# Another order of the stages for the second layer, and its weights loaded four pieces ahead, in a two-layer local-attention kernel

## The chip, the cores and the metric

The kernel runs on one core of one Trainium2 chip. The metric is the device time of one launch in microseconds (us), the median of several runs. Engines are called PE (TensorE; PEld is its loading of weights), DVE (VectorE), ACT (ScalarE), POOL (GpSimd) and SP (SyncE, which here only issues transfers). [...]

## What is computed

The input x is 8 sequences of 1024 tokens with 256 features, all in float32. Cut to what matters:

```python
x = layernorm(x + causal_attention(x, wq, bq, wk, bk, wv, bv, wo, bo))   # one head of 64
y = x
for l in range(2):                                 # two layers, 8 heads of 64, hidden width 682
    h = shift_token(y)                             # second half of the features from the token before
    q, k, v = split(h @ wqkv[l])
    q, k = rotary_xpos(l2norm(q) * q_scale[l], l2norm(k) * k_scale[l])
    o = local_attention(q, k, v)                   # a window of 128 tokens sees itself and the one before
    y = y + o @ wo[l]
    h = layernorm(shift_token(y)) * ln_g[l] + ln_b[l]
    a, g = split(h @ w1[l] + b1[l])
    y = y + (a * gelu(g)) @ w2[l] + b2[l]
x = layernorm(x + y)
```

## The kernel before

**Arithmetic.** To keep float32 accuracy, a matrix product is made of three passes: each operand is split into a high part (`hi`, a rounded copy by ACT) and the rest (`lo`, a subtraction by DVE or POOL), and hi*hi, hi*lo and lo*hi are added up in PSUM (`products`, L93). Weights are split once, by `split_weight` (L184 to L189), after a load into a staging tile.

**Three parts.** `fronts` runs the first attention for all sequences (to about 277 us). Then `layers` runs the two layers as one long loop, and the end of the loop is the end of the kernel. Layer 1 reads what layer 0 has written to DRAM (`x1_d`), and adds the input of layer 0 (`x0_d`) and the last layernorm.

**The loop.** Tiles of 128 tokens are numbered w = 0 to 127: 64 of layer 0, then 64 of layer 1. Round j (j = 0 to 66) works around w = 2j. It goes through a hand-written list, `ORDER`, whose entries are (stage, offset to w, and sometimes a half). The stages of a tile are:

- `prep` (once for two tiles): loads x (L670), transposes it (l_xp) and splits it (l_xT);
- `qk` (halves 0 and 1) and `v`: the projections l_pqk and l_pv; for `qk` the Square l_sq (L754) and its sum l_ss (L757), and the rotation l_t (L764, L771) with the table l_tab (L746); for `v` a copy l_v (L792);
- `unit`: the norms of q and k, a power on POOL (L144), and k's scaling (L782);
- `turn`: transposes q and k (l_t) into the ring of keys and queries;
- `sc`: the scores l_sc, their masked minimum on DVE (L843) and the exponential l_e on ACT (L703); after the second half the reciprocals of the denominators go to DRAM (L860) and come back spread over the partitions as `R` (L866);
- `et`: transposes l_e (eight transposes a half) and copies them, l_eT (L885);
- `val`: values times l_eT into one bank, l_po;
- `out`: l_on = l_po * R (L909), split into l_oT (L914, L915);
- `proj`: l_py, and its sum with x (L927).

After the `proj` of an odd tile, the feed-forward of the two tiles is put into a queue; each ("side", 1) in the list advances it by one of eleven steps: the shifted rows m_sh by transfers (L947 to L954) and the normalisation m_hn (L152, L153, L144, L964); the transposes m_hp; six steps m_pag with gelu on ACT (L703) and its product (L1013 to L1017); two steps m_pf; and the end, x (L1043), in layer 1 with the final norm o_st, o_mv (L1052). Both lists, old and new, have eleven sides.

**What sets the order on the engines.** The program text gives priorities; the Tile scheduler orders each engine's instructions at compile time, from the readiness that it simulates. On PE there is one more rule (`queued`, L114): the matmuls that use half of the array (`sc` and `val`) form groups that stay in program order with all the others before and behind them. Within a stretch between two such groups the scheduler is free. Buffers are counted by tag in `sizes`; "ps" (four banks) serves every PE result but the scores, which have four half-filled banks of their own ("sc").

**Weights of layer 1.** They share tiles with those of layer 0, one buffer each, so a split can start only when the last matmul of layer 0 that reads the old ones is done. Each piece is loaded into a staging tile of tag "sq", which is also that of the Squares, right where it is split: `load_qkv` when the first `prep` of layer 1 is traced (round 31), `load_wo` after the last `proj` of layer 0 (round 33), `load_w1` and `load_w2` inside the last feed-forward of layer 0. `load_b1` works out layer 1's b1 in rounds 1 and 2, and stages its pieces in "sq" too.

```python
        for j in range(PAIRS + 3):
            w = 2 * j
            if j >= 1:
                next(later, None)
            for item in ORDER:
                if item[0] == "side":
                    side(item[1])
                else:
                    run(item[0], w + item[1], *item[2:])
```

Of the kernel before, what the change touches and what calls it, by code (L numbers as in the profile page):

```python
# [9 lines left out]
FP = mybir.dt.float32  # L10
FR = mybir.dt.float32r
AF = mybir.ActivationFunctionType
ALU = mybir.AluOpType
# [13 lines left out]
def kernel(  # L27
# [544 lines left out]
    def load_w1(l, stage, W, ps=None):  # L572


        if ps is not None:
            b1_tiles(l, W)
        lgb, full = W["lgb"], NF * P
        W["w1"] = pair([P, 2, CW], "w1", wpool)
        gap = slice(2 * full + LEFT, 2 * full + OFF)
        for t in W["w1"]:  # L580
            nc.gpsimd.memset(t[:, :, gap].bitcast(FP), 0.0)
        for c in range(2):
            if ps is not None:
                pb = ps(f"pb1_{l}_{c}")
            for k, m0, m1, st in w1_parts(l, stage, c):
                if ps is not None:
                    b1_part(W, pb, c, k, m0, m1, st)
                nc.vector.tensor_scalar(st, st, lgb[:, 0, c : c + 1], None, ALU.mult)
                n = min(m1, NF) - m0
                s3 = st[:, 0 : n * P].rearrange("p (m q) -> p m q", q=P)  # L590
                d3 = [
                    t[:, c, 0 : 2 * full].rearrange("p (m k q) -> p m k q", k=2, q=P)[
                        :, m0 : m0 + n, k, :
                    ]
                    for t in W["w1"]
                ]
                split_weight(d3[0], d3[1], s3)
                if m1 > NF:
                    o = 2 * full + k * OFF
                    split_weight(  # L600
                        W["w1"][0][:, c, o : o + LEFT], W["w1"][1][:, c, o : o + LEFT],
                        st[:, n * P : n * P + LEFT],
                    )
                yield
            if ps is not None:
                b1_add(W, pb)

    def load_w2(l, stage, W):
# [22 lines left out]
        W["b2"] = b2t  # L631
        yield

    QB = 4
    PSB = {"ps": 4, "sc": 4}
    ORDER = [
        ("qk", 0, 0), ("unit", -2), ("unit", -1), ("side", 1), ("turn", -2, 0), ("side", 1),
# [4 lines left out]
        ("val", -2, 0), ("val", -2, 1), ("et", -1, 1), ("side", 1), ("qk", 1, 1),  # L642
        ("val", -1, 0), ("val", -1, 1), ("side", 1), ("side", 1), ("side", 1),
    ]

    def layers(pool, psum):
        sizes = {
            "sq": 4, "t": 6, "v": 4, "eT": 2, "oT": 2, "on": 1, "R": 2, "xT": 4, "hT": 2, "hn": 1,
            "sh": 3, "a": 10, "gl": 3, "x": 6, "tab": 2,
        }  # L650

        def tl(tag, shape, name, dt=FP):
            return pool.tile(shape, dt, tag=tag, name=name, bufs=sizes[tag])
# [3 lines left out]

        def sm(shape, tag, name, bufs=4, dt=FP):
            return pool.tile(shape, dt, tag=tag, name=name, bufs=bufs)

        def ps(name):
            return psum.tile([P, 512], FP, tag="ps", name=name, bufs=PSB["ps"])
# [274 lines left out]
        def feed_forward(l, b, p, x1, W):  # L937
# [82 lines left out]
            if change:  # L1020
                for _ in later:
                    pass
                for _ in load_w1(l + 1, stage, Ws[l + 1]):
                    pass
            py = ps(f"{nm0}_pf")
            for i in range(2):
                cols = slice(i * P, (i + 1) * P)
# [9 lines left out]
                passes(py[:, i * E : (i + 1) * E], steps)  # L1037
                yield
            if change:
                for _ in load_w2(l + 1, stage, Ws[l + 1]):  # L1040
                    pass
            xf = x1.rearrange("p t e -> p (t e)")
            nc.vector.tensor_tensor(xf, py, xf, ALU.add)  # L1043
            if not last_layer:
# [26 lines left out]
        def run(name, w, *args):  # L1071

            if not 0 <= w < DEPTH * B * NT:
                return
            l, b, t = w // (B * NT), w // NT % B, w % NT
            if (l, b) not in A:
                if "wqk" not in Ws[l]:
                    for _ in load_qkv(l, stage, Ws[l]):
                        pass
                W = Ws[l]  # L1080

                def finished(p, xt):
                    queue.append(feed_forward(l, b, p, xt, W))

                A[l, b] = attention(l, b, W, finished)
            A[l, b][name](t // 2 if name == "prep" else t, *args)
            if name == "proj" and b == B - 1 and t == NT - 1 and l + 1 < DEPTH:
                for _ in load_wo(l + 1, stage, Ws[l + 1]):
                    pass

        PAIRS = DEPTH * B * NT // 2
        group["on"] = True
# [15 lines left out]
        while queue:  # L1108
            side(1)

# [66 lines left out]
```

## Time and profile before

| What | Value |
| --- | --- |
| Median of 3 runs (lowest, highest) | 2683.63 us (2682.82, 2688.84) |
| The profiled execution's own time | 2688.53 us |
| Its span, first to last instruction | 2686.7 us |
| Mean granted clock of PE in it | 0.986 |
| PE, PEld busy | 2615.7 us, 2330.3 us |
| DVE, ACT, POOL busy | 2059.4, 1721.2, 1743.0 us |
| Matmuls | 22336 |

Times inside the kernel are those of one profiled execution, counted from its first instruction. Its own time is 1.8 us more than its span and 4.9 us more than the median. "L703" is line 703 of the kernel; a helper's line (L130 for every product, L133 for transposes, L90 and L91 for splits, L144 for powers) stands for many places, so tiles tell more than lines. In a list of waits, "PE l_et L133 <- ACT l_v L792" means that PE stood idle ahead of an l_et transpose until ACT's l_v copy was done; the numbers are the total, the count and the longest, in us. Matmuls are pipelined, so the times of neighbours overlap, and a matmul that starts late can still count as busy.

### The profile page before, as it was taken

Reading aid. Unit: us, or ns where it says so; the run is one execution under the profiler, and the core shown is the slowest. Engines: PE = TensorE matmul, PEld = TensorE weight load, DVE = VectorE, ACT = ScalarE, POOL = GpSimd, SP = SyncE. Lnnn points to the kernel's source line nnn. Section 1 sums busy time; section 2 is a strip of 40 time slices with the busy share of each in tenths; the row PEclk is TensorE's granted clock in tenths of the full one; section 3 lists DMA queues with packets and bytes.
Section 4 is the critical chain, followed back from the end, with each engine's and each line's share of the span. In section 5 each row is a group of like instructions: output and inputs, shape, how many; then the busy total and the mean of one; then the engine's idle time right before and its main releaser. Section 6 shows DMA issues by size and latency. Waiting matters only on the chain.

```text
span 2686.7 us, 61674 instructions
## 1 busy us (share of the span) xinstructions
PE 2615.7 (97%) x22336; PEld 2330.3 (87%) x22336; DVE 2059.4 (77%) x6304; ACT 1721.2 (64%) x4486; POOL 1743.0 (65%) x1996
## 2 busy tenths in 40 slices
PE   7998899999999999999999999999999999999997
PEld 5776799999999999999988888988888988889887
DVE  5787677777777777777778878887787877787775
ACT  5676466666666666666676666666666666666653
POOL 4565566666666666666666776676766767667673
PEclk8999899999999999999999999999999999999998
DMA  6332211111111111111121211111111111111110
GB/s 180 99 95 72 75 35 45 45 43 41 39 35 45 45 43 42 41 33 43 45 63 51 67 52 51 41 43 50 52 50 45 39 50 52 51 44 43 47 45 25
DMA packets 147265, 141.12 MB, mean 53 GB/s; under 512 B 28808, under 2 KB 123408, under 8 KB 146960
## 3 DMA queue, kind: packets, MB, share of 16 engines
q1 hardware_dynamic: 145600, 136.72, 17.4%
q8 instruction: 176, 2.88, 0.5%
q14 instruction: 129, 1.06, 0.1%
q10 hardware_dynamic: 1360, 0.46, 0.1%
HBM read 96.74 MB, written 27.81 MB: 46 GB/s over the span
## 4 chain that ended last, share of the span: by engine, by line
PE 65%; DVE 15%; POOL 8%; ACT 6%; issue 3%; DMA 2%; SPq 0%; POOLq 0%; DVEq 0%; ACTq 0%
PE m_pag L130 16%; PE l_pqk L130 10%; PE l_po L130 8%; PE l_et L133 6%; PE m_pf L130 6%; PE l_sc L130 4%; PE l_py L130 4%; PE l_pv L130 3%; ACT l_e L703 3%; PE l_t L133 3%; DVE l_t L764 2%; POOL l_t L771 2%; DVE l_ss L757 2%; DVE ring L91 2%; POOL l_oT L915 1%
## 5 line engine op out<-in xcount | busy, mean ns | idle before, releaser
L703 ACT ACTIVATE l_e<-l_sc,l_nm 128x256 f32<-128x256 f32 (+1 forms) x992 | 456.9, 481 | 216.8 <-DVE o_mv L153 107.7
L130 PE MATMUL m_pag<-m_hT,w_h 128*128 128x256 f32 (+1 forms) x2816 | 529.4, 288 | 0.7 <-ACT m_hT L90 0.7
L771 POOL TENSOR_TENSOR l_t<-l_t,l_t 128x256 f32<-128x256 f32 x512 | 369.8, 743 | 241.5 <-DVE l_t L764 241.5
L843 DVE CUSTOM_DVE_ANT_0 l_sc<-l_sc,mask,l_nrm_y 128x256 f32<-128x256 f32 (+1 forms) x1024 | 429.1, 466 | 45.8 <-ACT l_e L703 36.9
L130 PEld LDWEIGHTS m_pag<-m_hT,w_h 128*128 128x128 f32 (+1 forms) x2816 | 433.6, 188 | 17.7 <-issue 10.6
L703 ACT ACTIVATE m_gl<-m_pag,b 128x256 f32<-128x256 f32 (+1 forms) x384 | 181.9, 474 | 348.6 <-PE m_pag L130 348.5
L130 PE MATMUL m_pag<-m_hT,w_l 128*128 128x256 f32 (+1 forms) x1408 | 395.9, 281 | 0.0
L130 PE MATMUL l_pqk<-wqk_h,l_xT 128*128 128x512 f32 x1024 | 381.7, 414 | 1.4 <-ACT l_xT L90 0.8
L144 POOL TENSOR_TENSOR l_nrm_y<-l_nrm_a,half 128x16 f32<-128x16 f32 x128 | 373.6, 2918 | 10.5
L885 ACT COPY l_eT<-l_et 128x512 f32<-128x512 f32 (+1 forms) x512 | 274.5, 565 | 144.2 <-PE l_po L130 91.4
L764 DVE TENSOR_TENSOR l_t<-l_pqk,l_tab 128x512 f32<-128x512 f32 x512 | 327.3, 681 | 0.0
L1013 DVE SCALAR_TENSOR_TENSOR m_gl<-m_pag,b,m_gl 128x256 f32<-128x256 f32 (+1 forms) x384 | 183.6, 478 | 130.2 <-ACT m_gl L703 129.9
L133 PE MATMUL l_et<-ident,l_e 128*128 128x128 f32 x1920 | 266.3, 281 | 12.6 <-DVE l_cx L733 5.4
L1017 POOL TENSOR_TENSOR m_a<-m_gl,m_a 128x256 fp32r<-128x256 f32 x320 | 233.2, 735 | 54.3 <-DVE m_a L1016 53.0
L130 PEld LDWEIGHTS m_pag<-m_hT,w_l 128*128 128x128 f32 (+1 forms) x1408 | 264.0, 188 | 0.0
L133 PEld LDWEIGHTS l_et<-ident,l_e 128*128 128x128 f32 x1920 | 211.4, 141 | 58.6 <-DVE l_cx L733 12.5
L130 PE MATMUL m_pf<-w_h,m_a 128*128 128x256 f32 x1280 | 250.3, 282 | 0.0
L757 DVE TENSOR_REDUCE l_ss<-l_sq 128x8 f32<-128x512 f32 x256 | 175.1, 684 | 86.5 <-ACT l_sq L754 82.8
L130 PE MATMUL l_po<-l_eT,l_v 128*64 128x128 f32 x3840 | 239.5, 277 | 0.0
L130 PEld LDWEIGHTS l_po<-l_eT,l_v 128*64 128x64 f32 x3840 | 208.4, 137 | 34.1 <-issue 14.1
L142 POOL TENSOR_SCALAR l_nrm_a<-l_ss 128x16 f32<-128x16 f32 x128 | 32.3, 252 | 305.2 <-DVE l_ss L757 303.7
L130 PEld LDWEIGHTS l_pqk<-wqk_h,l_xT 128*128 128x128 f32 x1024 | 194.9, 190 | 38.1 <-DVE l_on L909 1.5
(168 smaller groups left out, 6704.8 us busy)
## 6 DMA issues: line engine op xcount, KB each, us to landing
l_R<-rd_d SPq DMA_DIRECT2D x256, 128.0 KB
x<-x_d SPq DMA_DIRECT2D x96, 256.0 KB
l_tab<-tab_d SPq DMA_DIRECT2D x128, 128.0 KB
xin<-in_L_attn_x_dram SPq DMA_DIRECT2D x16, 512.0 KB
x_d<-xin SPq DMA_DIRECT2D x16, 512.0 KB
rd_d<-l_rT SPq DMA_DIRECT2D x512, 1.0 KB
x_d<-x SPq DMA_DIRECT2D x32, 256.0 KB
out_dram<-x SPq DMA_DIRECT2D x32, 256.0 KB
```

The source lines that it names most:

```text
L91: nc.vector.tensor_tensor(lo, src, hi.bitcast(FP), ALU.subtract)
L130: queued(nc.tensor.matmul(*args, **kw), part)
L133: queued(nc.tensor.transpose(*args), False)
L144: nc.gpsimd.tensor_tensor(r, a, half.to_broadcast([P, n]), ALU.pow)
L703: ins = nc.scalar.activation(*args, **kw)
L757: nc.vector.tensor_reduce(st["ss", t][:, k * HEADS : (k + 1) * HEADS], sq.rearrange("p (g d) -> p g d", d=DH), AX.X, ALU.add)
L764: nc.vector.tensor_tensor(tt[j].rearrange("p (k h d) -> p k h d", k=2, d=DH), p3, tb.unsqueeze(2).to_broadcast([P, 2, HEADS // 2, DH]), AL ...
L771: nc.gpsimd.tensor_add(a[:, :, s, :], a[:, :, s, :], bsw[:, :, 1 - s, :])
L843: nc.vector.tensor_tensor_reduce(dst, dst, mk, st["nrm", w][:, 8 * u + h : 8 * u + h + 1], BIG, ALU.add, ALU.min, nm[:, one],)
L885: nc.scalar.copy(eT[:, j, 0:m], pt[:, 0:m])
L1013: nc.vector.scalar_tensor_tensor(gl[0:z, :], a_ps, W["b1"][0:z, 0, m : m + 1], gl[0:z, :], ALU.add, ALU.mult)
L1017: nc.gpsimd.tensor_tensor(a[1], gl[0:z, :], a[0].bitcast(FP), ALU.subtract)
```

## The change

Four things change, all in `layers`, beside new functions for the pieces.

1. A second list, `ORDER_1`, is used from round 33 on (`SWITCH`). In it a round's second tile gets its scores at the end of the round, and its `et`, `val`, `out` and `proj` in the next. At the switch two rounds of the new list are run without sides for what the old list has not yet done, which is `out` and `proj` of tile 62, and then two sides (`CATCH`). A set `done` keeps a stage from being run twice.
2. The weights of layer 1 are cut into 22 pieces (six of wqkv, two of wo, eight of w1, six of w2) by `parts_of`. Each is loaded into a tile of the new tag "ws", four buffers. The first four loads are issued after the `prep` of tiles 62 and 63 (round 30); later ones each when a piece before it is split. The splits stand where the whole loads stood.
3. To make room, "sq" has 2 buffers instead of 4, "R" 1 instead of 2, "sh" 2 instead of 3. This holds for both layers.
4. `load_b1` still stages in "sq".

```diff
+    def parts_of(l, W):
+        def from_rows(src):
+            def load(st):
+                nc.sync.dma_start(out=st, in_=src)
+            return load
+        def qkv(c, k):
+            def split(st):
+                if "wqk" not in W:
+                    t = pair([P, 2, 2, 2, INNER // 2], "wqk", wpool)
+                    W["parts"] = t
+                    W["wqk"] = [u.rearrange("p c g k f -> p c (g k f)") for u in t]
+                    W["wv"] = pair([P, 2, INNER], "wvv", wpool)
+                if k < 2:
+                    s3 = st.rearrange("p (g f) -> p g f", g=2)
+                    split_weight(*[u[:, c, :, k, :] for u in W["parts"]], s3)
+                else:
+                    split_weight(*[u[:, c, :] for u in W["wv"]], st)
+            src = wqkv[l, c * P : (c + 1) * P, k * INNER : (k + 1) * INNER]
+            return ("qkv", INNER, from_rows(src), split)
...
+        parts = [qkv(c, k) for c in range(2) for k in range(3)]
+        parts += [out_rows(c) for c in range(0, INNER // P, 2)]
+        cut = ((0, NF - 1), (NF - 1, NF + 1))
+        parts += [w1_piece(c, k, *m) for c in range(2) for k in range(2) for m in cut]
+        return parts + [w2_rows(m) for m in range(NF)] + [w2_left()]
+
+    SWITCH, CATCH = 33, 2
+    AHEAD = 2
+    ORDER_1 = [
+        ("side", 1), ("unit", -2), ("turn", -2, 0), ("turn", -2, 1), ("unit", -1), ("qk", 0, 0),
+        ("et", -3, 1), ("side", 1), ("et", -3, 0), ("sc", -2, 0), ("sc", -2, 1), ("val", -3, 0),
+        ("val", -3, 1), ("side", 1), ("qk", 0, 1), ("out", -3), ("turn", -1, 0), ("side", 1),
+        ("side", 1), ("proj", -3), ("turn", -1, 1), ("et", -2, 1), ("prep", 2), ("et", -2, 0),
+        ("v", 0), ("side", 1), ("qk", 1, 0), ("v", 1), ("side", 1), ("sc", -1, 0),
+        ("sc", -1, 1), ("val", -2, 0), ("val", -2, 1), ("side", 1), ("side", 1), ("side", 1),
+        ("side", 1), ("out", -2), ("qk", 1, 1), ("proj", -2),
+    ]
         sizes = {
-            "sq": 4, "t": 6, "v": 4, "eT": 2, "oT": 2, "on": 1, "R": 2, "xT": 4, "hT": 2, "hn": 1,
-            "sh": 3, "a": 10, "gl": 3, "x": 6, "tab": 2,
+            "sq": 2, "t": 6, "v": 4, "eT": 2, "oT": 2, "on": 1, "R": 1, "xT": 4, "hT": 2, "hn": 1,
+            "sh": 2, "a": 10, "gl": 3, "x": 6, "tab": 2, "ws": 4,
         }
+        loaded, to_come = [], []
+        def load_next():
+            if to_come:
+                name, width, load, split = to_come.pop(0)
+                st = tl("ws", [P, width], f"ws_{len(to_come)}_{name}")
+                load(st)
+                loaded.append((name, split, st))
+        def load_first(l):
+            to_come.extend(parts_of(l, Ws[l]))
+            for _ in range(sizes["ws"]):
+                load_next()
+        def take(name):
+            while loaded and loaded[0][0] == name:
+                _, split, st = loaded.pop(0)
+                split(st)
+                load_next()
...
-                for _ in load_w1(l + 1, stage, Ws[l + 1]):
-                    pass
+                take("w1")
...
-                for _ in load_w2(l + 1, stage, Ws[l + 1]):
-                    pass
+                take("w2")
...
-                    for _ in load_qkv(l, stage, Ws[l]):
-                        pass
+                    take("qkv")
...
-                for _ in load_wo(l + 1, stage, Ws[l + 1]):
-                    pass
+                take("wo")
+            if name == "prep" and b == B - 1 and t == NT - AHEAD and l + 1 < DEPTH:
+                load_first(l + 1)
+        done = set()
+        def one_round(order, w, sides):
+            for item in order:
+                if item[0] == "side":
+                    if sides:
+                        side(item[1])
+                    continue
+                stage = (item[0], w + item[1], *item[2:])
+                if stage not in done:
+                    done.add(stage)
+                    run(*stage)
         for j in range(PAIRS + 3):
             w = 2 * j
             if j >= 1:
                 next(later, None)
-            for item in ORDER:
-                if item[0] == "side":
-                    side(item[1])
-                else:
-                    run(item[0], w + item[1], *item[2:])
+            if j < SWITCH:
+                one_round(ORDER, w, True)
+                continue
+            if j == SWITCH:
+                for back in (4, 2):
+                    one_round(ORDER_1, w - back, False)
+                side(CATCH)
+            one_round(ORDER_1, w, True)
```

For comparison, the list of before, which stays in use up to round 32:

```python
    ORDER = [
        ("qk", 0, 0), ("unit", -2), ("unit", -1), ("side", 1), ("turn", -2, 0), ("side", 1),
        ("out", -4), ("turn", -2, 1), ("side", 1), ("out", -3), ("turn", -1, 0), ("sc", -2, 0),
        ("sc", -2, 1), ("turn", -1, 1), ("qk", 0, 1), ("side", 1), ("proj", -4), ("side", 1),
        ("sc", -1, 0), ("sc", -1, 1), ("et", -2, 0), ("qk", 1, 0), ("side", 1), ("proj", -3),
        ("v", 0), ("side", 1), ("prep", 2), ("v", 1), ("et", -2, 1), ("et", -1, 0),
        ("val", -2, 0), ("val", -2, 1), ("et", -1, 1), ("side", 1), ("qk", 1, 1),
        ("val", -1, 0), ("val", -1, 1), ("side", 1), ("side", 1), ("side", 1),
    ]
```

More of the change, by code (lines that the diff above doesn't have):

```diff
@@ L632, in load_w2, with out_rows, load, split @@
         yield
+    def parts_of(l, W):
[17 more added lines that the diff above has]
+            return ("qkv", INNER, from_rows(src), split)
+        def out_rows(c):
+            def load(st):
+                nc.sync.dma_start(
+                    out=st.rearrange("p (c e) -> p c e", c=2),
+                    in_=wo[l, c * P : (c + 2) * P, :].rearrange("(c p) e -> p c e", p=P),
+                )
+            def split(st):
+                if "wo" not in W:
+                    W["wo"] = pair([P, INNER // P, E], "wo", wpool)
+                split_weight(
+                    *[u[:, c : c + 2, :] for u in W["wo"]], st.rearrange("p (c e) -> p c e", c=2)
+                )
+            return ("wo", 2 * E, load, split)
+        def w1_piece(c, k, m0, m1):
+            full = NF * P
+            w = min(HID, m1 * P) - m0 * P
+            def split(st):
+                if "w1" not in W:
+                    W["w1"] = pair([P, 2, CW], "w1", wpool)
+                    for t in W["w1"]:
+                        nc.gpsimd.memset(
+                            t[:, :, 2 * full + LEFT : 2 * full + OFF].bitcast(FP), 0.0
+                        )
+                nc.vector.tensor_scalar(st, st, W["lgb"][:, 0, c : c + 1], None, ALU.mult)
+                n = min(m1, NF) - m0
+                d3 = [
+                    t[:, c, 0 : 2 * full].rearrange("p (m k q) -> p m k q", k=2, q=P)[
+                        :, m0 : m0 + n, k, :
+                    ]
+                    for t in W["w1"]
+                ]
+                split_weight(*d3, st[:, 0 : n * P].rearrange("p (m q) -> p m q", q=P))
+                if m1 > NF:
+                    o = 2 * full + k * OFF
+                    split_weight(
+                        *[t[:, c, o : o + LEFT] for t in W["w1"]], st[:, n * P : n * P + LEFT]
+                    )
+            o = k * HID + m0 * P
+            return ("w1", w, from_rows(w1[l, c * P : (c + 1) * P, o : o + w]), split)
+        def w2_rows(m):
+            def split(st):
+                if "w2" not in W:
+                    W["w2"] = pair([P, NF, E], "w2", wpool)
+                split_weight(*[t[:, m, :] for t in W["w2"]], st)
+            return ("w2", E, from_rows(w2[l, m * P : (m + 1) * P, :]), split)
+        def w2_left():
+            def load(st):
+                nc.vector.memset(st, 0.0)
+                for o in (0, OFF):
+                    nc.sync.dma_start(out=st[o : o + LEFT, :], in_=w2[l, NF * P : HID, :])
+            def split(st):
+                w2h = wpool.tile([P, E], FR, name=f"w2x_{l}", tag="w2x")
+                w2l = wpool.tile([P, E], FR, name=f"w2y_{l}", tag="w2y")
+                nc.gpsimd.memset(w2l.bitcast(FP), 0.0)
+                nc.scalar.copy(w2h, st)
+                nc.vector.tensor_tensor(
+                    w2l[0:LEFT, :], st[0:LEFT, :], w2h[0:LEFT, :].bitcast(FP), ALU.subtract
+                )
+                W["w2x"] = (w2h, w2l)
+                b2t = wpool.tile([P, E], FP, name=f"b2_{l}", tag="b2")
+                nc.sync.dma_start(out=b2t, in_=b2[l : l + 1, :].to_broadcast([P, E]))
+                W["b2"] = b2t
+            return ("w2", E, load, split)
+        parts = [qkv(c, k) for c in range(2) for k in range(3)]
[3 more added lines that the diff above has]
+        return parts + [w2_rows(m) for m in range(NF)] + [w2_left()]
@@ L644 @@
     ]
+    ORDER_1 = [
[6 more added lines that the diff above has]
+        ("side", 1), ("out", -2), ("qk", 1, 1), ("proj", -2),
+    ]
     def layers(pool, psum):
         sizes = {
-            "sq": 4, "t": 6, "v": 4, "eT": 2, "oT": 2, "on": 1, "R": 2, "xT": 4, "hT": 2, "hn": 1,
-            "sh": 3, "a": 10, "gl": 3, "x": 6, "tab": 2,
+            "sq": 2, "t": 6, "v": 4, "eT": 2, "oT": 2, "on": 1, "R": 1, "xT": 4, "hT": 2, "hn": 1,
+            "sh": 2, "a": 10, "gl": 3, "x": 6, "tab": 2, "ws": 4,
         }
```

## Prediction

> **What bounds the kernel now.** I read the page first, then the busy time by windows, then the waits of the tensor engine, then single stretches of the timeline. On the page, the lines of busy time and of the granted clock:
>
> ```profile
> PE 2615.7 (97%) x22336; PEld 2330.3 (87%) x22336; DVE 2059.4 (77%) x6304; ACT 1721.2 (64%) x4486; POOL 1743.0 (65%) x1996
> PE   7998899999999999999999999999999999999997
> PEclk8999899999999999999999999999999999999998
> ```
>
> PE is the bound: every slice but the first few and the last is at 9. What can still be won is PE time that is idle, or counted busy but slow. To see that, I took the start of the first Square of each round of the main loop as the round's start, and put four rounds (one sequence of eight tiles; the round that opens a sequence is shorter) side by side, layer 0 and layer 1:
>
> ```profile
> 1012.00:1157.90 145.90, 145.90 (x1290) 133.21 (x1289) 112.44 (x340) 96.19 (x248) 94.50 (x110) 1.00 0.14 41
> 2057.30:2206.10 148.80, 148.24 (x1290) 133.29 (x1290) 117.87 (x364) 96.18 (x249) 103.23 (x122) 1.00 0.16 48
> ```
>
> Columns: window, length, then busy us (and count) of PE, PEld, DVE, ACT, POOL, then clock, DMA share, GB/s. Both hold the same 1290 matmuls. Layer 0 needs 145.9 us with PE never idle: that is the floor, 36.5 us a round. Layer 1 needs 148.8: 2.9 us per four rounds, 0.73 a round, with 5.4 us more DVE and 8.7 more POOL work (the residual and final normalisation that only the last layer has). Only 0.56 of the 2.9 is idle PE; the rest hides in late matmuls. Starts summed by tile put 2.0 of the 2.8 that I find that way on the transposes l_et and 0.6 on l_xp. There are 28 such rounds, 1535.9 to 2577.5: 7 x 2.9 = **20 us** above the floor.
>
> The seam between the layers, round by round:
>
> ```profile
> 1376.50:1415.10 38.60, 37.59 (x331) 33.91 (x330) 30.74 (x87) 27.60 (x69) 24.26 (x26) 1.00 0.26 79
> 1415.10:1452.70 37.60, 37.48 (x330) 33.84 (x329) 29.64 (x87) 24.65 (x62) 26.83 (x33) 1.00 0.14 41
> 1452.70:1491.80 39.10, 37.12 (x307) 33.27 (x307) 28.45 (x86) 24.00 (x65) 25.45 (x30) 0.96 0.21 64
> 1491.80:1535.90 44.10, 39.35 (x331) 34.79 (x330) 38.34 (x103) 29.73 (x80) 31.51 (x41) 0.96 0.28 81
> ```
>
> The four are 159.4 long against 145.9: **13.5 us** lost. 7.9 of it is idle PE. The clock row takes about 4% of the last two, 3.3 us. The waits of PE from 1376 to 1536 name the cause:
>
> ```profile
> PE l_et L133 <- ACT l_v L792: 3.4, 3, 1.4
> PE l_et L133 <- DVE l_cx L733: 2.4, 1, 2.4
> ```
>
> Transposes find no free bank, because ACT and DVE, which empty the banks, stand in order behind weight splits. The ends of the run are not steady: PE is idle 11 us in the last 27, where one feed-forward runs alone.
>
> **The change, part by part.**
>
> *Weights ahead (seam).* The copies, subtractions and scalings stay: in the last seam window DVE has 38.3 us against about 29.8 in a layer-1 round, so 8.5 us of work for w1 and w2. What goes is the wait for loads (in the same windows ACT waits 1.8 us for st_wo, DVE 1.3 for st_w) and the staging through l_sq's buffers, which made Squares stand behind weights. Against that, DVE's 38.3 exceeds a 36.9 us round: at least 1.4 us cannot hide there, and the splits still come in bursts, in program order ahead of bank-emptying work. Bounds on the 13.5: all of it goes, or none and 2 us come from the four early loads, which SP issues in round 30 ahead of l_sh and l_tab (about 1 us of issue each, two of four exposed). I take 5 us left, the 1.4 plus about half of the 7.9 idle; saved **8.5**.
>
> The windows with a clock of 0.96 hold idle stretches of at most 2.4 us. [...]
>
> *The order (28 rounds).* ORDER has sc of both tiles close together, then et(-2,1) and et(-1,0), 16 transposes in a row, waiting for banks held by v's copy, xp's copy and eT's two buffers. ORDER_1 sets the two sc groups half a round apart, with val behind each, and moves one tile's et to the next round. So a transpose has, between its scores and itself, at least pf, qk, pf, proj (2.0+1.45+2.0+1.4 = 6.9 us of PE), against an exp burst of about 4.7 us in the timeline. The 0.73 should go: gain 28 x 0.73 = 20. Its cover for the bank-emptying is DVE, 29.5 of 37 us busy; per half round I count about 16 of 18 us in the half with the feed-forward's two norms, 14 in the other.
>
> But the new order shortens another chain, from the second proj of a pair to m_hp, since m_hp now has to come before sc(-1), and PE's queue keeps all unsplit matmuls ahead of the next sc group. Layer 1 in the timeline:
>
> ```profile
> 2112.60 0.28 PE L130 MATMUL l_py<-wo_h,l_oT 128*128 128x256 f32 x1
> 2114.17 0.41 DVE L927 TENSOR_TENSOR x<-l_py,x 128x256 f32<-128x256 f32 x1
> 2114.78 1.65 SPq L947 DMA_DIRECT2D m_sh<-x  x2
> 2117.73 0.49 DVE L152 BATCH_NORM_STATS2 m_st<-m_sh 128x6 f32<-128x128 f32 x2 [0.31 <-DMA m_sh<-x]
> 2118.94 0.71 POOL L144 TENSOR_TENSOR m_rs_y<-m_rs_a,half 128x2 f32<-128x2 f32 x1
> 2120.47 0.34 DVE L964 TENSOR_SCALAR m_hn<-m_sh,m_mv,m_rs_y 128x128 f32<-128x128 f32 x1
> 2121.26 0.64 PE L133 MATMUL m_hp<-ident,m_hn 128*128 128x128 f32 x4
> ```
>
> From the end of l_py (2112.85) to the end of m_hn (2120.81): 8.0 us, the same within 0.1 in twelve rounds of layer 1; 6.7 to 6.9 in three of four rounds of layer 0, where no final norm delays L927. In ORDER_1 the PE work between the two is turn 0.42, et 2 x 0.94, xp 0.5, v 2 x 1.42, qk 1.45 = 7.1 us. So the new stall is 0 (6.7) to 0.9 us a round (8.0); below 0 is excluded, since PE has no time to give back. The final norm comes closer ahead of L927 than now (pf ends only 1.4 us before), so neither end is safe; I take the middle, 0.45. Net: 28 x (0.73 - 0.45) = **8 us** saved. Bounds: 20 saved, or, with 0.9 plus 0.69 for one DVE instruction standing in front, 28 x (1.6 - 0.73) = 24 lost.
>
> *Smaller pools (layer 0 too).* R goes from 2 buffers to 1. Layer 0:
>
> ```profile
> 1072.66 1.25 SPq L866 DMA_DIRECT2D l_R<-rd_d  x2
> 1073.32 0.69 DVE L909 TENSOR_TENSOR l_on<-l_po,l_R 128x512 f32<-128x512 f32 x1 [0.25 <-PE l_po L130]
> 1078.63 0.68 DVE L909 TENSOR_TENSOR l_on<-l_po,l_R 128x512 f32<-128x512 f32 x1
> ```
>
> The second load must now wait for the first l_on, 1074.0 instead of 1072.66; issue 1.25 and about 1.3 to land (as l_sh from its issue's end to L152) give 1076.6, needed at 1078.6. Nothing, with 2 us of cover; behind it on SP stands only the next l_tab, 6 us later. If the cover went, it would be up to 1 us in 32 rounds. [...] sq from 4 to 2: Squares are 7 to 10 us apart in a round and each is read within 1.4 us: nothing. But the two early rounds that compute b1 stage four pieces each through sq; with two buffers a second wave of load and matmul follows, 0 to 3 us a round, about half under other work: **+2**. sh from 3 to 2: one per round, nothing.
>
> *Switch and end.* Round 33 only pulls out(62) and proj(62) forward; all PE work is the same in sum. The last feed-forward alone stays the end. 0, within 3 either way (nearest row: 11 us idle in the last 27).
>
> Sum: -8.5 - 8 + 2 = -14.5. The profiled execution took 2688.5 (span 2686.7 and 1.8 around it), 4.9 above the median of 2683.6; it would be 2674. On the median: **2669**.
>
> **Rivals.** About 0.2%, 5.4 us, is what a measurement of this kernel can tell from no change.
>
> (a) Everything is covered: steady rounds at the floor and the seam nearly whole, -20 - 12 + 1: 2653. For it: layer 0 proves that PE can be full with two po banks held, and ORDER_1 holds one less. Against: the 8.0 us chain. Chance 0.10.
>
> (b) The stall only moves: 0.73 a round becomes as much at m_hp, and the seam alone gains: -8.5 + 2 = 2677, straddling the bound. For it: 8.0 against 7.1. Chance 0.15.
>
> (c) Slower: m_hp becomes the round's limit. One more DVE instruction (0.69) before L927 or m_hn makes the stall 1.6 us, +24 - 6.5: 2701. It decides once the stall exceeds 0.73 + 6.5/28 = 0.96 us, a chain of 8.06, just over today's. For it: that half has DVE at 16 of 18 us. Against: sc(-1)'s eight DVE operations, which now stand near this chain, come after it in the new order. Chance 0.23.
>
> (d) One R buffer holds up layer 0, 1 us x 32 less the 14.5: 2701. Against: 2 us of cover. Chance 0.04.
>
> **How the numbers follow.** The forecast, 2655 to 2678, has 0.48. Faster: 0.46 of it, all of (a), 0.05 of (b): 0.61. Within the bound: 0.02 and 0.10: 0.12. Slower: (c) and (d), 0.27. With both signs possible the range reaches from (a), with 3 us of the end's uncertainty, 2650, to (c), 2701; beyond lie about half of (c) and (d) and little below.
>
> **What would show it.** Four layer-1 rounds: 147.7 us in the forecast, 145.9 in (a), 149 in (b), 152 in (c). The waits should name m_hp <- m_hn in place of l_et. The four seam rounds: about 151, clock 1.00. Layer 0's four rounds stay at 145.9; (d) would show there. If l_et still waits for l_cx or l_v in layer 1, my account of the order is wrong.

## The result, and the profile after

| | Before | Changed |
| --- | --- | --- |
| Median of 7 runs each (lowest, highest) | 2683.36 us (2681.6, 2688.84) | 2694.07 us (2687.97, 2696.28) |
| Ratio, 95% interval | 1 | 1.0032 (1.0021 to 1.0043) |
| Span of the profiled execution | 2686.7 us | 2692.2 us |

The changed kernel is slower by 0.32%; 2669 was forecast, so the prediction is wrong in sign. The spans differ by 5.5 us and the medians by 10.7, since the profiled execution before was 5.2 us above its median and the one after is at its own (2694.07); so places are compared by the profile and totals by the medians. Cut by the rounds (start of a round's first Square to the next, as in the prediction), the two executions and those of two experiments read:

| us | Before | Changed | Old order, weights ahead | New order, old loads |
| --- | --- | --- | --- | --- |
| ahead of round 0 | 276.9 | 278.9 | 274.0 | 275.5 |
| rounds 0 to 2 | 77.5 | 77.9 | 78.4 | 77.3 |
| rounds 3 to 30 | 1022.2 | 1020.0 | 1020.6 | 1020.8 |
| rounds 31 to 35 (seam) | 196.8 | 201.1 | 192.0 | 203.1 |
| rounds 36 to 62 | 1004.2 | 1003.5 | 1005.4 | 1003.0 |
| from round 63 to the end | 109.2 | 110.8 | 110.3 | 111.7 |

The first row is the same code in all, between 267.9 and 278.9 in the runs of this study: it is scatter. What the change touches is the seam (+4.3), the steady rounds (-0.7) and the end (+1.6); 8.5 and 8 us had been booked as gains in the first two. These three add up to 5.2 us (6.9 against a second profile of the kernel before, e12), and the medians differ by 10.7: the other 4 to 5 us stand in no place that the profiles of single executions show.

On the page, busy time, PE's slices and the clock look much as before (PE is even 11 us less busy); the page alone would not show the loss:

```profile
PE 2604.8 (97%) x22336; PEld 2332.9 (87%) x22336; DVE 2065.4 (77%) x6304; ACT 1724.3 (64%) x4486; POOL 1737.5 (65%) x1996
PE   7988899999999999999999999999999999999997
PEclk8999899999999999999999999999999999999998
```

**The seam.** The busy time by windows, the four rounds 31 to 34 (columns as in the prediction):

```profile
1376.80:1414.40 37.60, 37.40 (x330) 33.86 (x330) 30.47 (x85) 27.64 (x68) 24.11 (x26) 1.00 0.24 75
1414.40:1459.10 44.70, 43.34 (x381) 39.66 (x380) 35.45 (x100) 27.77 (x69) 31.46 (x39) 1.00 0.12 36
1459.10:1496.60 37.50, 33.06 (x253) 29.33 (x252) 29.08 (x86) 21.46 (x58) 20.65 (x24) 0.95 0.17 53
1496.60:1540.90 44.30, 38.67 (x331) 33.93 (x330) 36.97 (x99) 30.29 (x80) 31.63 (x40) 1.00 0.24 73
```

They are 164.1 us long, against 159.4 before and 151 in the forecast. The second holds 51 more matmuls and the third 54 fewer, since the switch pulls work forward; so they are read as a pair. In the third and the fourth PE is idle for 4.4 and 5.6 us. The waits of PE in this stretch have a new name at the top; the l_et waits for l_v and l_cx of before are gone:

```profile
PE m_hp L133 <- DVE m_hn L1102: 6.6, 4, 2.7
PE l_t L133 <- DVE l_t L902: 2.6, 2, 1.3
```

The timeline of round 33 shows how DVE comes to be late with m_hn:

```profile
1467.72 0.28 PE L130 MATMUL l_py<-wo_h,l_oT 128*128 128x256 f32 x1
1468.71 0.68 DVE L91 TENSOR_TENSOR ring<-l_t,ring 128x512 fp32r<-128x512 f32 x1
1469.31 0.41 DVE L1065 TENSOR_TENSOR x<-l_py,x 128x256 f32<-128x256 f32 x1
1474.06 1.09 DVE L687 TENSOR_SCALAR ws_w<-ws_w,lgb 128x512 f32<-128x512 f32 x1 [2.10 <-DMA ws_w<-in_L_ffn_w_dram]
1475.07 0.47 DVE L152 BATCH_NORM_STATS2 m_st<-m_sh 128x6 f32<-128x128 f32 x2
1475.89 0.68 DVE L895 TENSOR_REDUCE l_ss<-l_sq 128x8 f32<-128x512 f32 x1
1476.19 0.71 POOL L144 TENSOR_TENSOR m_rs_y<-m_rs_a,half 128x2 f32<-128x2 f32 x1
1476.48 1.28 DVE L902 TENSOR_TENSOR l_t<-l_pqk,l_tab 128x512 f32<-128x512 f32 x2
1477.84 1.43 POOL L909 TENSOR_TENSOR l_t<-l_t,l_t 128x256 f32<-128x256 f32 x2 [0.94 <-DVE l_t L902]
1477.93 0.74 DVE L1102 TENSOR_SCALAR m_hn<-m_sh,m_mv,m_rs_y 128x128 f32<-128x128 f32 x1
1478.07 0.33 PE L133 MATMUL m_hp<-ident,m_hn 128*128 128x128 f32 x1 [2.71 <-DVE m_hn L1102]
```

l_py ends at 1468.00. The sum with x starts 1.3 us later, behind rotations and a ring split. Then the scaling of a w1 piece (L687) stands in DVE's queue ahead of m_st and waits 2.1 us for its load; l_ss and two l_t (2.0 us) stand ahead of m_hn; most of that passes while POOL works out m_rs_y, which m_hn needs too, and 0.8 us of it comes behind m_rs_y's end at 1476.90. Two of the four m_hn take 0.74 and 0.76 us, where the others take 0.34. From l_py's end to that of m_hn it is 11.6 us, against the 8.0 that the prediction carried over from the steady rounds and the 6.6 of a regular round of the new order. Of the 5.0 us over the latter, 1.3 are the late sum, 2.4 lie between it and m_st (SP issues l_R and a weight load ahead of the second m_sh, and then comes the scaling), 0.7 come from l_ss and l_t, and 0.8 from the slow m_hn (0.2 are won back on the way to m_rs_y). Round 34 is alike, with other splits in front: m_hn ends 12.2 us after l_py (PE idle 1.89 and 0.96 us at m_hp).

**The steady rounds.** Four rounds of layer 0, then three sequences of layer 1:

```profile
1013.50:1159.20 145.70, 145.70 (x1290) 133.17 (x1289) 112.55 (x340) 96.08 (x248) 94.41 (x110) 1.00 0.14 42
1652.00:1801.20 149.20, 147.47 (x1291) 133.71 (x1290) 117.73 (x364) 96.29 (x249) 102.54 (x123) 1.00 0.15 47
2098.70:2248.50 149.80, 147.35 (x1290) 133.71 (x1289) 117.73 (x364) 96.42 (x249) 102.59 (x123) 1.00 0.16 47
2396.70:2544.40 147.70, 146.54 (x1290) 133.70 (x1289) 117.95 (x364) 96.22 (x248) 102.47 (x122) 1.00 0.16 48
```

The last is 147.7 us, the forecast's own number; the two others are 1.5 and 2.1 longer at the same work. The waits of PE over the whole steady stretch, 1640 to 2550:

```profile
PE l_pqk L130 <- DVE m_gl L1151: 5.5, 13, 0.6
PE l_t L133 <- ACT m_gl L841: 1.7, 7, 0.3
PE m_hp L133 <- DVE m_hn L1102: 1.7, 4, 0.8
```

No l_et is left, so the new order did what the account of it said. Two others came: l_pqk for m_gl, in the round that opens a sequence, and m_hp in a few rounds. By length, the regular rounds went from 37.5 to 36.97 us, the opening ones from 36.28 to 36.73, and nine rounds stand out at 0.3 to 1.7 us over their kind.

A regular and a long round next to each other, the timeline of rounds 50 and 51:

```profile
2111.76 0.28 PE L130 MATMUL l_py<-wo_h,l_oT 128*128 128x256 f32 x1
2112.53 1.65 SPq L1085 DMA_DIRECT2D m_sh<-x  x2
2115.40 0.49 DVE L152 BATCH_NORM_STATS2 m_st<-m_sh 128x6 f32<-128x128 f32 x2
2118.80 0.60 PE L133 MATMUL m_hp<-ident,m_hn 128*128 128x128 f32 x4
...
2148.72 0.28 PE L130 MATMUL l_py<-wo_h,l_oT 128*128 128x256 f32 x1
2149.48 1.65 SPq L1085 DMA_DIRECT2D m_sh<-x  x2
2154.26 0.49 DVE L152 BATCH_NORM_STATS2 m_st<-m_sh 128x6 f32<-128x128 f32 x2 [1.95 <-DMA m_sh<-x]
2156.69 1.01 PE L133 MATMUL m_hp<-ident,m_hn 128*128 128x128 f32 x4 [0.83 <-DVE m_hn L1102]
```

Up to the issue of m_sh the two agree within 0.02 us. Then m_st starts 2.87 us after the start of the issues in the one and 4.78 in the other. In the regular round m_hp follows the last m_hn with 0.1 to 0.2 us to spare; so any delay beyond that lengthens the round. The DMA view of 2149.4 to 2154.3, the time of the late transfer, has packets on two queues named "instruction", of which that of the regular round shows none:

```profile
q1 hardware_dynamic: 444, 0.28, 20.4%
q8 instruction: 1, 0.02, 1.8%
q14 instruction: 1, 0.01, 0.4%
```

The packet on q8 is 16 KB long and takes 1.41 us from 2151.68 on, the one on q14 is 8 KB and takes 0.31. The expectations below call such a packet an instruction fetch; the trace tells no more of it than the name of its queue, its size and its time.

### The profile page after: what moved, and what is told of

Same layout as the page of the kernel before. It is cut to its first block, busy times and chain, and to the rows that moved or that the text cites. A ratio compares the mean times of both kernels' runs of the same rounds, so it can differ in the third digit from the quotient of the medians.

```text
span 2692.2 us, 61664 instructions
## 1 busy us (share of the span) xinstructions
PE 2604.8 (97%) x22336; PEld 2332.9 (87%) x22336; DVE 2065.4 (77%) x6304; ACT 1724.3 (64%) x4486; POOL 1737.5 (65%) x1996
## 4 chain that ended last, share of the span: by engine, by line
PE 82%; DVE 7%; ACT 5%; DMA 3%; POOL 2%; issue 1%; SPq 0%; POOLq 0%; ACTq 0%; DVEq 0%
PE m_pag L130 15%; PE l_pqk L130 12%; PE m_pf L130 10%; PE l_po L130 8%; PE l_et L133 7%; PE l_sc L130 7%; PE l_py L130 6%; PE l_pv L130 5%; PE l_t L133 4%; ACT l_e L841 2%; PE f_sc L130 1%; DMA m_sh<-x 1%; PE f_pz L395 1%; DVE l_t L902 1%; PE m_hp L133 1%
## 5 line engine op out<-in xcount | busy, mean ns | idle before, releaser
L909 POOL TENSOR_TENSOR l_t<-l_t,l_t 128x256 f32<-128x256 f32 x512 | 368.8, 741 | 138.9 <-DVE l_t L902 138.9
L841 ACT ACTIVATE m_gl<-m_pag,b 128x256 f32<-128x256 f32 (+1 forms) x384 | 175.3, 474 | 284.8 <-PE m_pag L130 242.0
L1053 POOL TENSOR_TENSOR l_oT<-l_on,l_oT 128x512 fp32r<-128x512 f32 x128 | 165.1, 1290 | 257.9 <-ACT l_oT L1052 257.9
L1023 ACT COPY l_eT<-l_et 128x512 f32<-128x512 f32 (+1 forms) x512 | 268.4, 569 | 69.1 <-PE l_po L130 39.9
L133 PE MATMUL l_et<-ident,l_e 128*128 128x128 f32 x1920 | 254.1, 277 | 3.0 <-ACT l_v L930 1.6
L130 PE MATMUL m_pf<-w_h,m_a 128*128 128x256 f32 x1280 | 256.2, 286 | 0.0
L130 PE MATMUL l_po<-l_eT,l_v 128*64 128x128 f32 x3840 | 239.1, 277 | 0.9 <-ACT l_eT L1023 0.9
```

The lines of the kernel that those rows point to most:

```text
L130: queued(nc.tensor.matmul(*args, **kw), part)
L133: queued(nc.tensor.transpose(*args), False)
L841: ins = nc.scalar.activation(*args, **kw)
L909: nc.gpsimd.tensor_add(a[:, :, s, :], a[:, :, s, :], bsw[:, :, 1 - s, :])
L1023: nc.scalar.copy(eT[:, j, 0:m], pt[:, 0:m])
L1053: nc.gpsimd.tensor_tensor(oT[1], on, oT[0].bitcast(FP), ALU.subtract)
```

## The experiments

The ratios below are to the kernel before, run on the same chip beside each.

### The parts by themselves

**e1: old order, the rest of the change.**

```diff
-    SWITCH, CATCH = 33, 2
+    SWITCH, CATCH = 1000, 2
```

> The old list in every round, with the weights four pieces ahead and the smaller pools. Theory 1 (the loss is the transposes m_hp, which in the new list have no slack behind the chain from the second l_py over the transfer m_sh to m_hn): without the new list m_hp no longer stops PE at the seam, and loading ahead is left alone; the four seam rounds take 150 to 155 us (159.4 before, 164.1 after), four steady rounds of layer 1 148.8; in all 4 to 9 us faster than before. Theory 2 (the splits' work itself, DVE fuller than a round, costs the time wherever it stands): the seam stays at 158 to 164, in all within 3 us of before. Theory 3 (the smaller pools cost): layer 0 is longer than 145.9 in four rounds and the whole not faster than before.

2680.31 us, 0.9989 (0.9979 to 0.9998). The seam takes 192.0 us, 4.8 less than before; rounds 36 to 62 are as before but for round 39, which is 0.9 us longer. This is a gain of 0.1%, 3.2 us where theory 1 had 4 to 9, and together with e9 the fastest form in the study that computes the same. Of PE's waits in rounds 31 to 35 the longest are

```profile
PE l_t L133 <- DVE l_t L902: 1.2, 1, 1.2
PE l_sc L130 <- ACT l_e L841: 1.2, 1, 1.2
```

and m_hp is not among them.

**e2: the new order from round 33, with the old loads and the old pools.**

```diff
+            if j < SWITCH:                       # on the kernel before, its loads and sizes kept
+                one_round(ORDER, w, True)
+                continue
+            if j == SWITCH:
+                for back in (4, 2):
+                    one_round(ORDER_1, w - back, False)
+                side(CATCH)
+            one_round(ORDER_1, w, True)
```

> The new list from round 33 on, with the weights loaded and staged as before and the pools of before. Theory 1: m_hp still stops PE at the seam (6 us or more idle) and in those steady rounds where an instruction fetch falls on m_sh; steady rounds 147.7 to 150 in four, the seam 162 or more; in all 5 to 15 us slower than before. Theory 2: the seam is as before, 159; in all within 3 us of before. Theory 3: faster than the changed kernel by all of its loss, 8 to 11 us.

2694.28 us, 1.0037 (1.0024 to 1.0051): the whole loss, without the loads and without the small pools. Its seam takes 203.1 us, with 6.0 us of waits of m_hp for m_hn.

**e4: the kernel before with the three small pools, and e8: the same with l_sq's four buffers kept.**

```diff
-            "sq": 4, ... "R": 2, ... "sh": 3,
+            "sq": 2, ... "R": 1, ... "sh": 2,      # e4;  e8 keeps "sq": 4
```

> The kernel before with sq 2, R 1 and sh 2 buffers alone. Theories 1 and 2: within 2 us of before, with 0 to 3 us more in rounds 1 and 2 and a seam that is up to 5 us longer, since two staging tiles serve the weights instead of four. Theory 3: 5 to 10 us slower, layer 0 longer than 145.9 in four rounds.

2698.55 us, 1.0061 (1.0049 to 1.0073); the seam takes 210.7 us, where one wait stands out:

```profile
PE l_po L130 <- DVE l_t L764: 8.1, 1, 8.1
```

Here the whole weights are still staged in "sq", so two buffers are dear; in the changed kernel they are cheap only because the pieces have tiles of their own.

> The kernel before with R 1 and sh 2, but sq at 4: tells which of the smaller pools made the last four-pool run 15 us slower, all of it at the seam. If it was sq, which stages the weights there: within 2 us of before. If R or sh: 5 us slower or more.

2687.6 us, 1.0018 (1.0008 to 1.0029), some 4 us slower; the seam takes 196.5 us, as before. Round 1 is 36.24 us there and 32.75 before, with 7.3 us of idle PE. Why, I can't say.

**e9: e1 with two buffers of R.**

```diff
-    SWITCH, CATCH = 33, 2
+    SWITCH, CATCH = 1000, 2
-            "sq": 2, ... "R": 1,
+            "sq": 2, ... "R": 2,
```

> The old list in every round, the weights four pieces ahead, sq 2 and sh 2, but R back at 2: the part of the change that was found to gain, without the pool that an earlier run leaves in doubt (R 1 and sh 2 alone: 4 us slower). If R is what costs there: 3 to 5 us faster than with R 1, 6 to 8 faster than before. If R is free, as its rows say: within 2 us of the run with R 1, about 3 us faster than before.

2679.66 us, 0.9989 (0.9977 to 1.0000), against 2680.31 for e1: a second R buffer is worth nothing that can be measured. Rounds 3 to 30, all of layer 0, take 1020.1 us with two and 1020.6 with one.

**e12: the kernel before once more.**

> The kernel before once more, for a second profile of it: its first profiled run took 2688.5 us, 5 above its median. All theories: its rounds 31 to 35 at 195 to 198 us and rounds 38 to 62 at 930.4 to 932, with the 5 us in the part before the loop and in its first rounds.

2685.18 us, 1.0005 (0.9992 to 1.0018); seam 195.2, rounds 38 to 62 930.7 us (930.4 in the first profile). So a seam is told to about 2 us, a steady stretch to about 0.5.

### Is it m_hp, and what makes it late

**e3: the side that holds m_hp moved behind `val`(-2).**

```diff
-        ("v", 0), ("side", 1), ("qk", 1, 0), ("v", 1), ("side", 1), ("sc", -1, 0),
+        ("v", 0), ("side", 1), ("qk", 1, 0), ("v", 1), ("sc", -1, 0),
-        ("side", 1), ("out", -2), ("qk", 1, 1), ("proj", -2),
+        ("side", 1), ("side", 1), ("out", -2), ("qk", 1, 1), ("proj", -2),
```

> The changed kernel with one side moved in the new list: the step that issues m_hp stands behind val of tile -2, and so behind the scores, which gives the chain about 3.5 us more before PE needs it. Theory 1: no more idle PE for m_hp; the irregular steady rounds (6.8 us in 28 rounds) and the 6.6 us at the seam with its slow clock (1.7) go: 12 to 15 us faster than the changed kernel, 2 to 6 faster than before. Theory 2: within 3 us of the changed kernel.

2809.25 us, 1.0465 (1.0451 to 1.0478): a clear miss. m_hp no longer waits, but what reads it does, by the waits from 1640 to 2550:

```profile
PE m_pag L130 <- ACT m_hT L90: 58.7, 22, 3.9
```

m_hT is cast by ACT, and it now stands in ACT's queue behind the burst of exponentials of `sc`(-1); each round is 41.4 us long. The place of m_hp ahead of the scores is needed: the burst behind it is what it must not get behind.

**e7: the half `qk`(1, 1) moved ahead of that side, as cover.**

```diff
-        ("v", 0), ("side", 1), ("qk", 1, 0), ("v", 1), ("side", 1), ("sc", -1, 0),
+        ("v", 0), ("side", 1), ("qk", 1, 0), ("v", 1), ("qk", 1, 1), ("side", 1), ("sc", -1, 0),
-        ("side", 1), ("out", -2), ("qk", 1, 1), ("proj", -2),
+        ("side", 1), ("out", -2), ("proj", -2),
```

> The changed kernel with the stage (qk, 1, 1) of the new list moved from behind the scores of tile -1 to ahead of m_hp: 1.45 us more PE work between the second l_py and m_hp. If the steady irregular rounds come from m_sh landing late behind an instruction fetch, with no slack to hide it, they shrink by up to 1.45 us each: 27 steady rounds (36 to 62) go from 1003.5 to about 998, the idle time for m_hp at the seam from 6.6 to about 3.5; in all 8 to 10 us faster than the changed kernel. If they have another cause: the same as the changed kernel, or slower where one bank more is held ahead of the scores.

2703.28 us, 1.0083 (1.0069 to 1.0098). No m_hp waits from 1640 to 2560 (from 1300 to 1640, with the seam, 5.2 us are left, where 3.5 were expected), but the proj at the end has lost its cover:

```profile
PE l_py L130 <- DVE m_gl L1151: 27.3, 25, 1.6
```

The regular rounds grow to 37.83 us. This order has 1.45 us of PE work to place, and two spots that want it.

**e10 and e11: no token shift in the feed-forward, in the changed kernel and in the one before.**

```diff
-            sh = tl("sh", [P, 2, P], f"{nm0}_sh")
-            for r0, r1 in ((1, 113), (113, P)):
-                nc.sync.dma_start(out=sh[r0:r1, :, :], in_=x1[r0 - 1 : r1 - 1, :, P:E])
...
+            sh = x1[:, :, P:E]
```

> The changed kernel with the token shift of the feed-forward left out (its output is another): the transfers m_sh and last_d are gone, and the norm reads x itself. This takes some 2.3 us and every landing out of the chain from l_py to m_hn. Theory (chain plus instruction fetches): no idle PE for m_hp in steady rounds, none of the irregular rounds, rounds 38 to 62 at 922 to 924 us (929.4 in the changed kernel); at the seam 4 to 8 us less; in all 11 to 16 us faster than the changed kernel, and faster than the old list without the shift by 5 us or more. If the irregular rounds have another cause: they stay, and at most 4 us are won.

> The kernel before with the same transfers left out, as the other run's partner. The old list has m_hp 0.4 us or more behind m_hn and its stalls elsewhere (l_et behind l_cx), so the theory expects rounds 38 to 62 within 2 us of 930.4, and in all 0 to 4 us faster than before. If the chain over m_sh bounds the old list as well: 10 us faster or more.

New order 2678.29 us, 0.9984 (0.9973 to 0.9995); old order 2678.83 us, 0.9984 (0.9972 to 0.9997). In the steady rounds 38 to 62 the new order goes from 929.4 to 924.95 us and its long rounds are gone; the old one stays (931.2, from 930.4). That carries the reading of the long rounds: they come through m_sh. The new order's regular rounds, at 37.2 us, are 0.2 longer than with the shift, which I can't explain; so it is less than the 922 to 924 that were expected. Some 6 us of both totals are won at the end (110.8 to 105.0 and 109.2 to 103.1), where the last feed-forward runs alone. At the seam it was a miss. The new order's is 201.2 us as ever, and the waits there hardly move:

```profile
PE m_hp L133 <- DVE m_hn L1092: 6.5, 4, 2.4
```

So the transfer is not what makes m_hn late at the seam; by the timeline of round 33, what is left is DVE's own queue. I had also expected the new order to come out 5 us ahead of the old one; it didn't, since the seam took it.

### Switch or weights

**e5 and e6: the switch at round 37, behind all weights, or at round 21, in layer 0.**

```diff
-    SWITCH, CATCH = 33, 2
+    SWITCH, CATCH = 37, 2        # e6: 21, 2
```

> The changed kernel with SWITCH 37 in place of 33: the weights are split under the old list, the new list begins three rounds after the last split. Theory A (at the seam the splits and loads of the weights lengthen the chain from l_py to m_hn, and the new list has no slack for it): rounds 31 to 35 as with the old list throughout, 192 us, the switch itself costs 2 us or less, the steady rounds stay at 147.7 plus what the instruction fetches add; in all 10 to 13 us faster than the changed kernel. Theory B (the switch itself, its catch-up rounds, costs the time): 4 us or more of idle PE move to rounds 37 and 38, in all 4 to 6 us faster than the changed kernel.

2686.13 us, 1.0009 (0.9996 to 1.0021). The seam is that of e1, 192.2 us; rounds 36 and 37, where the switch now is, take 79.96 us and took 73.78 before: +6.2, with 2.8 us of it at m_hp. The loss moved with the switch. The total lies between the two theories, 7.9 us under the changed kernel.

> The changed kernel with SWITCH 21: the new list begins twelve rounds ahead of the weights, in layer 0. Theory A: idle PE before m_hp stays in rounds 33 and 34, rounds 31 to 35 take 198 us or more; nothing of that in rounds 21 to 24; layer 0's rounds under the new list are within 0.3 us of the old ones but where a fetch falls on m_sh and in those that open a sequence (36.7 for 35.1); in all within 4 us of the changed kernel. Theory B: rounds 31 to 35 at 192, the loss at rounds 21 and 22.

2705.20 us, 1.0079 (1.0064 to 1.0095); both theories missed. Rounds 20 and 21 take 80.3 us instead of the changed kernel's 71.95, +8.4; the nine rounds of layer 0 behind it 338.3 instead of 328.3, 1.1 each; and the seam 200.2 us although no switch is in it. Four rounds of that seam still run layer 0's feed-forward, so up to 4.4 of its 8.2 us over e1 can be that price; what is left stands beside the weights. So the new order is dear in three places: where it starts, in layer 0, which had no stall to lose, and beside the weights.

**e13 and e14: the second layer's weights neither loaded nor split, with the new order from round 33 and with the old one.**

```diff
-                if "wqk" not in Ws[l]:
-                    take("qkv")
+                for key in ("wqk", "wv", "wo", "w1", "w2", "w2x", "b2"):
+                    Ws[l].setdefault(key, Ws[0][key])
-            if name == "prep" and b == B - 1 and t == NT - AHEAD and l + 1 < DEPTH:
-                load_first(l + 1)
...
-    SWITCH, CATCH = 33, 2
+    SWITCH, CATCH = 1000, 2      # e14 alone
```

> The changed kernel with the second layer's weights left out: they are neither loaded nor split, and layer 1 computes with layer 0's. The order still switches at round 33. It tells whether the loss at the seam (rounds 31 to 35, floor about 184 us of the columns, 201.1 in the changed kernel) comes from the splits that stand ahead of m_hn in VectorE's queue or from the switch of order itself. Theory A (the splits and the scaling that waits for its load stand ahead of m_hn): rounds 31 to 35 take 190 to 193 us, 6 to 8 over the twin run with the old order, and of it only the switch's own 6 to 8 us as when the switch stood at round 37; the waits of m_hp fall from 6.6 us to under 3. Theory B (the new order alone makes m_hp late there, splits or not): 196 us or more, with m_hp still waiting over 5 us. Theory C (the switch costs nothing without weights beside it): within 2 us of the twin.

> The twin: the same with the second layer's weights left out, and the old order throughout. Rounds 31 to 35 take 185 to 188 us by all theories, since nothing stands beside them that the regular rounds (37.5 and 36.28 us) do not have; against it the new order's run is read. The time is some 5 us under the old order with weights ahead (2680.3), so about 2675.

2682.32 us, 0.9980 (0.9968 to 0.9992), and 2672.11 us, 0.9949 (0.9933 to 0.9966). With the twin the seam is a table of two orders by three treatments of the weights, rounds 31 to 35 in us:

| | No second weights | Loaded ahead | Old loads |
| --- | --- | --- | --- |
| Old order | 183.1 | 192.0 | 196.8 |
| New order | 189.3 | 201.1 | 203.1 |
| Difference | 6.2 | 9.1 | 6.3 |

The busy time by windows: rounds 32 and 33 together under the old order, then round 33 under the new one:

```profile
1410.30:1482.20 71.90, 71.90 (x634) 65.64 (x633) 55.92 (x170) 47.31 (x124) 47.31 (x56) 1.00 0.14 42
1455.30:1490.80 35.50, 32.04 (x256) 28.22 (x255) 27.36 (x83) 20.32 (x57) 19.28 (x23) 1.00 0.15 42
```

The old order has no idle PE at all there; the new one has 3.5 us in one round, 2.6 of it at m_hp:

```profile
PE m_hp L133 <- DVE m_hn L1102: 2.6, 2, 1.6
```

In that round of e13, DVE does l_ss, two l_t and a ring split ahead of the sum with x, which starts 1.3 us after l_py has ended, and l_ss and two l_t once more ahead of m_hn, as in the changed kernel. In a regular round (44) the first four are done before l_py ends, and the others come behind m_hn. No weight stands between. m_hn ends 10.1 us after l_py, 3.5 later than in a regular round: 1.3 from the late sum, 1.1 from l_ss and two l_t behind m_rs_y, 0.8 from slow m_hn, the rest on the way to m_st. So theory A holds (189.3 lies just under its 190 to 193, as 183.1 lies under the twin's 185 to 188): the switch costs 6.2 us by itself. Of it 3.7 us are idle PE; some 1.4 of the rest, by the numbers of matmuls started in rounds 31 to 35 under the two orders (22 m_pag, 12 l_py, 8 l_t more; 13 l_et, 32 l_po fewer; an estimate at some 0.11 us each, from the 145.7 us of 1290 matmuls in layer 0's four rounds, and half that for l_po, of which 3840 are busy for 239.1 us), are work done earlier; the last 1.1 count as busy PE and were not traced further. The end, 111.5 against 108.7 us, gives none of it back.

## Why the prediction was wrong, step by step

| Term | Forecast, us | Measured, us | From |
| --- | --- | --- | --- |
| Weights ahead, seam, old order | -8.5 | -4.8 (-3.2 against e12) | e1 and before |
| Switch and end | 0 (within 3) | +6.2 for the switch, +1.6 at the end | e14, e13, e5; before and changed |
| Weights beside the new order | not seen | +2.9, told to about 2 | 9.1 less 6.2; e6 has some too |
| Steady order | -8 | -0.7 | rounds 36 to 62 |
| sq in the rounds with b1 | +2 | +0.4, within scatter (77.3 to 79.9 in all runs) | rounds 0 to 2 |
| R | 0 | 0 | e9 against e1 |
| sh | 0 | not run alone; e8's 4 us are open | e8 |

**Seam: the size of what stays.** "I take 5 us left". Under the old order, rounds 31 to 34 are 154.6 us, 8.7 above the floor of 145.9; without weights they are 145.6. So the floor was right and the 8.7 is the price of the weights that is left when they are loaded ahead, which I had put at 1.4 plus half of the idle time. Loading early takes away most of the waiting for loads (DVE still waits 0.9 us for ws_w in e1), not the queueing behind splits on DVE and ACT.

**Seam: the step that failed.** "Round 33 only pulls out(62) and proj(62) forward; all PE work is the same in sum." The sum of work is the same, and it is not what counts: at the switch DVE's order differs from the steady one, and m_hn comes 3.5 us late in one round (e13), with the weights beside it 5.0 and 5.6 us in two. So a term put at 0 measured +6.2. The prediction had worked out the chain from l_py to m_hp, 8.0 us against 7.1 us of cover, and applied it to the 28 steady rounds only. It belonged to the rounds of the transition, too. There DVE is no busier than elsewhere (29.1 of 37.5 us in round 33, about 29.6 of 37 in a regular round); what differs is what stands in front. The same working (0.69 us for each DVE instruction in front) would have pointed there: l_ss, two l_t and a ring split ahead of the sum are 2.8 us by that price, of which 1.3 came behind l_py's end. The same goes for the splits, which it said would stand "in program order ahead of bank-emptying work", and did not put ahead of m_hn.

**Steady: mechanism right, size wrong.** The l_et waits are gone, m_hp takes some of their place, and the undisturbed sequence is at 147.7. Of rounds 36 to 62, the 20 regular ones gained 0.53 each (10.6), the seven opening ones lost 0.45 each (3.1), and what the long ones have over their kind is 6.8. I had "neither end is safe" for the chain's length, and took the middle; the regular chain is in fact 6.6 us, since the final norm of the pair before, which had made it 8.0, moved behind the sum with x. So the cover just suffices, with 0.1 to 0.2 us to spare, and those rounds, at 36.97 us against 36.87 in layer 0, are nearly rival (a). What undid it are the late m_sh transfers, for which the prediction had no term. The old order is not safe from them either: its regular rounds have m_hp 0.4 us behind m_hn, and where a transfer is late, in round 39 of e1, e4, e9 and e14, the round is 0.9 to 1.2 us longer. In the kernel before none is late in these rounds, in the changed one eight are. Why so many more fall together under the new order, no run shows. Rival (b), "the stall only moves", is what the steady part came to, by another mechanism.

**What would show it.** Layer 0's four rounds, 145.7, and the absence of l_et are as announced; the clock of 1.00 at the seam is not: 0.95 in round 33.

**The slower rivals.** (c), m_hp as the limit of every round, did not come; (d) did not either: over 28 rounds of layer 0, one R buffer against two makes 0.5 us (1020.6 in e1, 1020.1 in e9). The chance for slower had the right engine and the right tile, in the wrong rounds: a switch priced at zero was no rival at all.

## What to carry to other kernels

Price a change of order at the place where it begins, too: the transition runs through each engine's queue in an order that is neither the old nor the new one, and its chains (here l_py to m_hn) must be worked out with what is queued there, instruction by instruction. A schedule that is exactly covered in the median round has not won yet: ask how much spare the chain has against a transfer that lands a microsecond late. And when two edits come together, run each alone: here the loads gained 0.1% and the order lost 0.4%.

## What the runs showed of the hardware

**Packets on the queue "instruction" go with late transfers.** Packets of 16 KB on this queue come about every 15 us (176 in the changed kernel's execution, median 1.0 us long). In the changed kernel's rounds 38 to 61, m_st starts 2.2 to 2.3 us after the second m_sh issue has started; in seven rounds in which such a packet falls into that transfer it takes 2.75 to 4.07, and the round is 0.34 to 1.74 us longer. One more round (44) is 0.43 long without such a packet; there the first m_sh was issued 0.6 us late. In other runs the packets fall elsewhere: in the kernel before and in e12, none falls into an m_sh transfer in rounds 36 to 62, and none of these rounds is long; under the old order in e1, e4, e9 and e14 one does, in round 39, the transfer takes 3.3 to 3.6 us, and the round is 0.9 to 1.2 longer. This is agreement in time over many rounds and runs, and still not an experiment: no run moved the packets and nothing else. How a packet would hold up the transfer was not shown.

**m_hn is twice as long behind an operation of POOL.** It takes 0.34 us in the median of the changed kernel's 256 instances, and 0.74 to 0.76 in the four that start while POOL's sum of l_t (L909) is running. In 66 more, an operation of POOL starts while m_hn is running, and these keep 0.33 to 0.35. Before, the three that start during one of POOL's take 0.77 to 0.79. The operations of POOL that they start behind take 0.72 to 0.76 us. Why m_hn is longer there was not shown. Where such a pair falls is a matter of the order, so an order that puts l_t ahead of m_hn pays here as well.

**Half a clock after short gaps.** Behind the idle 2.71 and 1.02 us that end at 1478.07 and 1479.41 comes a stretch of 3.4 us at half the clock from 1480.4 on, with PE busy. In the kernel before, gaps of 1.44 and 0.54 us went ahead of such a stretch (half the clock for 3.4 us from 1477.79). The length of a gap alone does not tell it: behind 1.89 and 0.96 us in round 34, and behind 1.56 and 1.02 in e13, the clock stayed whole.
